# Moving sums, gates, products and evictions by one or two tiles in a kernel with a hand-made order of issue

## The chip, the cores and the metric

One Trainium2 chip, one core of it. The metric is the device time of one execution in microseconds, as the median of several runs. The engines are TensorE (PE, with its weight loads as PEld), VectorE (DVE), ScalarE (ACT), GpSimd (POOL) and SyncE (SP), which issues nearly all DMAs. Each engine works through its own instructions in the order in which the program issued them; between engines there are only semaphores. So the order of issue is a part of the kernel, and it is what changes here.

## What is computed

Four layers follow one another on an image of 4 x 192 x 64 x 64, all in f32. The change touches the first two, which are built around a selective scan (Mamba). Cut to what matters:

```python
# layer 0: tokens of 192 channels, 4096 in each image
xs = layernorm(x.reshape(b, -1, c), ln_g, ln_b)
y1 = mamba(xs, m1...)                  # two mambas over the same tokens,
y2 = mamba(flip(xs, -1), m2...)        # the second with its channels turned round
out = xs + y1 + y2

def mamba(x, ...):                     # 384 inner channels, 16 states
    xc, z = split(x @ in_w.T)
    xc = silu(causal_conv(xc) + conv_b)          # 4 taps (3 in layer 1)
    dt, B, C = split(xc @ x_w.T)
    dt = softplus(dt @ dt_w.T + dt_b)
    h = exp(dt * A) * h + (dt * xc) * B          # over the 4096 tokens
    y = sum(h * C, states) + D * xc
    return (y * silu(z)) @ out_w.T

# layer 1
x1 = x + mamba(layernorm(x))
x2 = x1 + gelu(batchnorm(depthwise3x3(x1)))
out = x2 + mlp(layernorm(x2))                    # 192 -> 768 -> 192, gelu
```

Layers 2 and 3 (a convolution with weights from a squeeze, windows multiplied in sedenions, an MLP) come after and are untouched.

## The kernel before

**Units, halves, tiles.** The tokens are worked in chunks of 512. In the first stage (`two_mambas`, layer 0) a unit is one chunk of one image, 32 units in all, and each has two halves, one for each mamba. In the second stage (`mamba_block`, layer 1) a unit has one mamba. For one mamba and one chunk, 384 channels times 16 states give 48 scans of 128 x 512, and these are the tiles: 12 groups k of 4 tiles j. A tile is one `tensor_tensor_scan` on VectorE (L636), for which ScalarE makes the decay `dA` two tiles ahead (L630, three buffers in PSUM). For each group there is a product dtx * B before the scans (L623: on VectorE, but on GpSimd for groups 3, 7 and 11 of the first stage, the `shared` ones, whose B is a copy in SBUF named Bs), and afterwards a product h * C on GpSimd (L649, in `read`).

**What follows the scans.** `sum` (L653) adds the 16 states up with four products into one PSUM tile `y` (L658); four groups make one `y` of 128 channels, c = k // 4, and there is a single buffer for it (`psum_y`). In the first stage the fourth sum also adds D * xc (L668), and `Mamba.skip` then is the gate: it multiplies `y` with silu(z) on VectorE into `m_y` (L681), and `Mamba.gate` does nothing. In the second stage `skip` adds D * xc (L683) and `gate` multiplies on GpSimd. `Scans.step` enters these for later tiles with `at(...)` (L776 to L783), counted from the last tile of a group. With the third gate of a half `gated` is set, and after the second mamba the output products (`back`, L877) are added.

**Work behind the scans.** All the rest, the norms, the fronts of the next unit, the outputs, the depthwise convolution and the MLP, is issued in small pieces between the tiles by `Behind`. Four lanes hold generators; at each tile `tick` lets the lanes go on as far as the rules allow. A `Piece` says what its step costs TensorE (`pe`, taken from a budget that grows by a fixed price for each tile), how many tiles must pass first (`wait`), which other steps must be done (`after`), whether it takes one of the two PSUM banks (`bank`), and whether it is a `burst`: one long activation with another function table, which is let in only at an edge, a tile whose number is 1 modulo 4 and that is not followed by a shared group's product. What empties a bank is entered with `later` and issued some tiles afterwards:

```python
    def later(self, fn, dve=False, bank=True, more=0, act=0.65):
        done = [False]
        due = self.now + (self.dve if dve else self.act) + more
```

The first stage has `Behind(psum, 1.6, 2, 3, 1.0)`: a TensorE budget of 1.6 us a tile, evictions on ScalarE two tiles later, on VectorE three, and 1.0 us of ScalarE's time a tile. The second has `Behind(psum, 1.8, 1, 2, 1.4)` (L1019). Where something is needed and not yet issued, `force` issues everything at once until it is there: `rows` (dt and dt * xc written to DRAM, from where SyncE loads them spread over the partitions), C and Bs, `silu`, `y_free`.

**A front** (`Mamba.front`, L462) is the chain of one mamba and chunk: products `ps_in`, the convolution, a burst silu(xc) (L488), the products `ps_x` (L489 to L492), `ps_dt`, a burst softplus (L512), dt and dt * xc to DRAM, the products for z and a burst silu(z) (L530). A lane works one front after the other, each during the half before its own.

**The norm of the first stage** (`norm` in `two_mambas`, L834) makes 12 short passes on ScalarE (L845) with a few small steps on GpSimd between, then transposes on TensorE (`ps_t`, L863) into `xT`, which has two buffers. `back` of the unit before still reads the older one. It starts once `last`, the output of the unit before (`added`), is done (L916 to L918).

**Second stage:** `NormT.run` (L302) makes a norm with products for mean and variance and a product that spreads 1/sigma (`rb`), multiplied in on VectorE (L347). `MlpT.run` (L366) makes six hidden products, a burst gelu and two outputs of six products (`ps_o`), which VectorE adds to the image (`last`, L1150). `tail` (L1103) makes the depthwise convolution as 18 products (`ps_dw`, L1115) with an eviction on ScalarE (L1124) for each of two halves of the channels and then a burst gelu (L1134).

Of the kernel before, what the change touches and what calls it, by code (L numbers as in the profile page):

```python
# [285 lines left out]
class NormT:  # L286
# [15 lines left out]
    def run(self, x, g, b, d, which):  # L302
        nc, behind = self.nc, self.behind
        nq = T // 128
        mean = behind.bank([CP, T], "mean")
        for k in range(2):
# [5 lines left out]
            dve=True,  # L312
# [25 lines left out]
        for q in range(nq):  # L338
# [10 lines left out]
            ),  # L349
            dve=True,  # L350
        )
        for k in range(2):
# [6 lines left out]
class MlpT:  # L359
# [6 lines left out]
    def run(self, x, taken, last):  # L366
# [22 lines left out]
        for k in range(2):  # L389
            for m in range(NH):  # L390
                if m % 2 == 0:
                    yield Piece(1.7, bank=m == 0, wait=0 if m or k else 2)
                if m == 0:
                    ps = behind.bank([CP, T], "ps_o")
                nc.tensor.matmul(  # L395
                    ps,
                    self.w2[:, m, bass.ts(k, CP)],
                    h[:, m, :],
                    start=(m == 0),
                    stop=(m == NH - 1),  # L400
                )
            h_last = behind.later(lambda k=k, ps=ps: last(k, ps), dve=True)
        yield Piece(after=[h_last])
# [15 lines left out]
class Mamba:  # L419
# [42 lines left out]
    def front(self, xn, first, u):  # L462
# [25 lines left out]
        nc.scalar.activation(xc, xc, AF.Silu)  # L488
        yield Piece(2.6, bank=True, wait=2)  # L489
        ps = behind.bank([RK + 2 * NS, T], "ps_x")  # L490
# [111 lines left out]
    def spread_C(self, u, o):  # L602

        for n, i in (("C", 2 + o), ("Bs", o)):
            if n == "Bs" and not any(k % 2 == o for k in self.shared):
                return
            if n == "Bs":
                yield Piece(0.85, bank=True)
            v = self.work.tile([128, T], F32, name=f"{n}{o}", bufs=2 if n == "C" else 1)
            ps = self.behind.bank([128, T], f"ps_{n}")  # L610
            self.nc.tensor.matmul(ps, self.ex.spread[:, i, :], u["dbl"], start=True, stop=True)
            done = self.behind.later(lambda v=v, ps=ps: self.nc.scalar.copy(v, ps))  # L612
            yield Piece(after=[done])
            u[n, o] = v
# [79 lines left out]
class Scans:  # L694
# [21 lines left out]
    def run(self):  # L716
# [10 lines left out]
        for i in range(self.AHEAD):  # L727
            m.decay(u, 0, i)
        for i in range(n + 16):
            if i < n:  # L730
                self.step(i, n)
            for fn in self.due.pop(i, []):
                fn()
            self.behind.tick(self.edge(i + self.AHEAD, n))
# [6 lines left out]
    def step(self, i, n):  # L741
# [24 lines left out]
        if j == 3:  # L766
# [5 lines left out]
            if i + 1 < n:  # L772
                m2, u2, k2, _ = self.tile(i + 1)
                if k2 not in m2.shared:
                    m2.product(u2, k2)
            late = 2 if m.shared else 0  # L776
            self.at(i + 4 + late, lambda: self.sum(m, u, k))
            if k % 4 == 3:
                c = k // 4
                self.at(i + 6 + late, lambda: self.skip(m, u, c))  # L780
                self.at(i + 8, lambda: m.gate(u, c))
                if c == ND - 1:
                    self.at(i + 8, lambda: self.gated(u, after))  # L783

# [17 lines left out]
def two_mambas(tc, x, gb_ap, m_ins, ex_aps, out, at_first):  # L802
# [3 lines left out]
    with ExitStack() as ctx:  # L806
# [26 lines left out]

        def norm(u):  # L834
            xt = u["x"]
# [23 lines left out]
            for k in range(2):  # L859
                yield Piece(1.1, bank=True, wait=1)  # L860
                ps = behind.bank([CP, T], "ps_t")
# [49 lines left out]
        for n, u in enumerate(units):  # L911
            following = units[n + 1] if n + 1 < len(units) else None

            def before(i, n=n, u=u, following=following):
                if i == 0 and following:
                    load(following)  # L916
                    last = [units[n - 1]["added"]] if n else []
                    behind.add(3, norm(following), Piece(wait=3, after=last))  # L918
                if following:
# [76 lines left out]
def mamba_block(tc, x, p96, p96_ap, p128, p128_ap, m_in, ex_aps, out, sums, following):  # L996
# [4 lines left out]
    with ExitStack() as ctx:  # L1001
# [16 lines left out]

        behind = Behind(psum, 1.8, 1, 2, 1.4)  # L1019
        ln = NormT(nc, const, work, behind)  # L1020
# [82 lines left out]
        def tail(b, t):  # L1103
# [4 lines left out]
            for k in range(2):  # L1108
                for j in range(9):
                    if j % 3 == 0 and (j or k):  # L1110
                        yield Piece(2.6, bank=j == 0)
                    if j == 0:
# [16 lines left out]
                            bias=bn_t[:, k : k + 1],  # L1129
                        )  # L1130
                    )
# [699 lines left out]
```

## Time and profile before

| | us |
|---|---|
| median of 9 runs | 10762.62 (10743.57 to 10771.31) |
| the profiled execution: its time | 10761.38 |
| its span, first to last instruction | 10759.3 |
| first stage, two mambas on each chunk | about 0 to 5380 |
| second stage, one mamba, convolution, MLP | about 5380 to 8830 |
| layers 2 and 3 | to the end |

Busy times by stage (us in the stretch; clock is the share of TensorE's full clock that was granted):

| stretch | PE | DVE | ACT | POOL | clock |
|---|---|---|---|---|---|
| 200 to 5380 (5180 us) | 4215.7 | 4932.3 | 3489.9 | 4658.2 | 0.80 |
| 5700 to 8600 (2900 us) | 2627.4 | 2571.6 | 1997.5 | 2063.4 | 0.88 |
| 8900 to 10760 (1860 us) | 1565.8 | 945.9 | 738.6 | 197.8 | 0.91 |

The stages are so regular that a gap on an engine comes back in each unit at the same place. A group of instructions is read as: line, engine, operation, what it writes and reads, count, then busy time, mean ns of one, and the engine's idle time just before these instructions with what ended it.

### The profile page before, as it was taken

The page shows a single profiled execution, that of the slowest core. Times are in us where ns is not written, and L with a number is a line of the kernel's source. Part 1 is how long each engine was busy: PE and PEld are TensorE (multiplying, and loading weights), DVE is VectorE, ACT ScalarE, POOL GpSimd, SP SyncE. Part 2 cuts the span into 40 slices and gives each one's busy share as a digit, 9 for nine tenths or more (in the row PEclk, how much of TensorE's full clock was granted, in tenths as well). Part 3 has the DMA queues.
Part 4 walks back from the last instruction along what each step waited for, and adds up shares of the span by engine and source line. Part 5 has one row for each costly group of instructions (what it writes and reads, how often), then busy time and mean ns, then how long its engine had stood idle before and what let it go on. Part 6 is the DMA issues. An engine that isn't in the chain of part 4 may idle for free. (4 is left out here: it accounts for less than half of the span.)

```text
span 10759.3 us, 97520 instructions
## 1 busy us (share of the span) xinstructions
PE 8998.6 (84%) x30776; PEld 3510.5 (33%) x30776; DVE 9037.7 (84%) x7697; ACT 6652.8 (62%) x9626; POOL 7363.4 (68%) x3584
## 2 busy tenths in 40 slices
PE   7888888888888888888668999989999986889898
PEld 2222222222222222222223333333333333455455
DVE  7999999999999999999968888888888875555552
ACT  5666666666666666666546767666666653444433
POOL 6889898988888989889857677767677751111100
PEclk7888787878877878788767888889888887899999
DMA  6666666666666666666545555555555542112110
GB/s 166 173 180 183 173 176 174 184 174 173 180 176 174 176 175 185 172 173 180 156 127 141 142 140 147 141 141 148 135 147 139 145 109 72 43 49 64 43 40 18
DMA packets 969562, 1515.13 MB, mean 141 GB/s; under 512 B 244346, under 2 KB 277150, under 8 KB 968534
## 3 DMA queue, kind: packets, MB, share of 16 engines
q1 hardware_dynamic: 968190, 1505.85, 52.5%
q8 instruction: 245, 4.01, 0.2%
q10 hardware_dynamic: 856, 3.05, 0.1%
q14 instruction: 271, 2.22, 0.1%
HBM read 1295.45 MB, written 213.12 MB: 140 GB/s over the span
## 5 line engine op out<-in xcount | busy, mean ns | idle before, releaser
L636 DVE TENSOR_TENSOR_SCAN h<-dA,m_state,h 128x512 f32<-128x512 f32 x3840 | 4659.6, 1266 | 378.7 <-ACT dA L630 310.0
L649 POOL TENSOR_TENSOR h<-h,C 128x2048 f32<-128x2048 f32 x960 | 4348.6, 4530 | 77.7
L630 ACT ACTIVATE dA<-dtE,m_A 128x512 f32<-128x512 f32 x4608 | 3086.5, 686 | 1300.9 <-DVE h L636 1193.5
L623 DVE TENSOR_TENSOR h<-dtxE,B 128x2048 f32<-128x2048 f32 x960 | 2171.1, 2262 | 69.9 <-DMA dtxE<-r_dtx 69.9
L658 PE MATMUL y<-h,gather 128*32 128x512 f32 x7680 | 1266.7, 739 | 461.4 <-POOL h L649 276.1
L474 PE MATMUL ps_in<-xT,m_in_w 96*128 96x512 f32 x1536 | 1109.7, 866 | 193.7 <-ACT z L481 171.6
L1366 POOL TENSOR_TENSOR d<-d,rs 128x512 f32<-128x512 f32 x64 | 86.4, 1350 | 1600.4 <-DVE rs L1365 1579.9
L648 POOL COPY m_state<-h 128x4 f32<-128x4 f32 x960 | 183.1, 191 | 1161.6 <-DVE h L636 1152.1
L636 DVE TENSOR_TENSOR_SCAN h_apart<-dA,m_state,h_apart 128x512 f32<-128x512 f32 x768 | 924.3, 1260 | 39.8 <-ACT dA L630 39.7
L623 POOL TENSOR_TENSOR h_apart<-dtxE,Bs 128x2048 f32<-128x2048 f32 x192 | 882.4, 4596 | 36.7 <-ACT Bs L612 29.2
L649 POOL TENSOR_TENSOR h_apart<-h_apart,C 128x2048 f32<-128x2048 f32 x192 | 869.7, 4529 | 15.5
L548 PE MATMUL ps_conv<-raw,m_conv 128*128 128x512 f32 x1536 | 720.9, 612 | 0.0
L474 PEld LDWEIGHTS ps_in<-xT,m_in_w 96*128 96x128 f32 x1536 | 375.9, 267 | 942.7 <-issue 407.0
L1115 PE MATMUL ps_dw<-strip,dw 96*96 96x512 f32 x1152 | 590.6, 662 | 3.4 <-ACT x L1124 0.9
L658 PEld LDWEIGHTS y<-h,gather 128*32 128x32 f32 x7680 | 168.0, 117 | 1283.0 <-POOL h L649 568.7
L474 PE MATMUL ps_in<-xn,m_in_w 96*128 96x512 f32 x768 | 441.0, 719 | 164.4 <-ACT z L481 70.5
L492 PE MATMUL ps_x<-xc,m_pack 128*44 128x512 f32 x576 | 340.8, 739 | 230.2 <-ACT xc L488 190.7
L395 PE MATMUL ps_o<-hid,t 128*96 128x512 f32 x768 | 446.4, 729 | 75.3 <-ACT ln_rs L332 66.1
L1531 PE MATMUL sed_ps<-xn,sed 64*128 64x256 f32 (+3 forms) x2944 | 486.3, 403 | 7.0 <-DVE y L1550 7.0
L630 ACT ACT_TABLE_LOAD x345 | 442.6, 1283 | 14.7 <-DMA dtE<-r_dt 8.6
L548 PEld LDWEIGHTS ps_conv<-raw,m_conv 128*128 128x128 f32 x1536 | 286.6, 195 | 439.3 <-issue 356.1
L376 PE MATMUL ps_h<-xn,t 96*128 96x512 f32 x768 | 394.8, 661 | 30.6 <-ACT hid L381 16.8
(202 smaller groups left out, 12210.9 us busy)
## 6 DMA issues: line engine op xcount, KB each, us to landing
dtE<-r_dt SPq DMA_DIRECT2D x2304, 256.0 KB, 5.1
dtxE<-r_dtx SPq DMA_DIRECT2D x2304, 256.0 KB, 4.3
r_dt<-dt SPq DMA_DIRECT2D x96, 768.0 KB, 4.0
r_dtx<-raw SPq DMA_DIRECT2D x96, 768.0 KB, 6.4
x<-x SPq DMA_DIRECT2D x64, 384.0 KB, 3.9
img<-x SPq DMA_DIRECT2D x28, 512.0 KB, 9.1
xt<-in_x SPq DMA_DIRECT2D x32, 384.0 KB, 6.3
x<-o SPq DMA_DIRECT2D x32, 384.0 KB, 2.6
```

What stands on the lines that cost most here:

```text
L376: nc.tensor.matmul(ps, self.w1[:, k, bass.ts(m, 128)], x[:, k, :], start=(k == 0), stop=(k == 1))
L395: nc.tensor.matmul(ps, self.w2[:, m, bass.ts(k, CP)], h[:, m, :], start=(m == 0), stop=(m == NH - 1),)
L474: nc.tensor.matmul(ps, self.in_w[:, k, bass.ts(e, 128)], xn[:, k, :], start=(k == 0), stop=(k == 1))
L492: nc.tensor.matmul(ps, self.x_w[:, d, :], xc[:, d, :], start=(d == 0), stop=(d == ND - 1))
L548: nc.tensor.matmul(ps, self.conv[:, d, j, :], raw[:, d, j : j + T], start=(j == 0), stop=(j == K - 1))
L623: engine.tensor_tensor(h, u["rows", k // 2, 1], u[B, k % 2].unsqueeze(1).broadcast_to([128, 4, T]), ALU.mult)
L630: self.nc.scalar.activation(dA, u["rows", k // 2, 0][:, j, :], AF.Exp, scale=self.A[:, k, j : j + 1])
L636: self.nc.vector.tensor_tensor_scan(h[:, j, :], u.pop(("dA", k, j)), h[:, j, :], self.state[:, k, j : j + 1], ALU.mult, ALU.add,)
L649: nc.gpsimd.tensor_tensor(h, h, u["C", k % 2].unsqueeze(1).broadcast_to([128, 4, T]), ALU.mult)
L658: self.nc.tensor.matmul(u["ys"][32 * j : 32 * j + 32, :], self.ex.gather[:, i // 2, :], h[:, j, :], start=(i == 0), stop=(i == 3 and not s ...
L1115: nc.tensor.matmul(ps, dw[:, k, j, :], s[:, k, dy : dy + rows, dx : dx + HW], start=(j == 0), stop=(j == 8),)
L1531: nc.tensor.matmul(out, sed[p, int(h is not None), i ^ position(k, s), cols], xn[b, g][p, c, :], start=group(t) not in begun, stop=left[gr ...
```

## The change

Nothing that is computed changes, only where it is issued:

- In the first stage the sum of a group is issued 7 tiles after its last scan (it was 6), the gate 10 (it was 8), and `gated`, which lets the output products and z's buffer go, 10 (it was 8). In the second stage these numbers stay as they were. The loop of tiles runs four turns longer for it.
- `ps_x`, which follows the burst silu(xc), waits 4 tiles in the first stage and 3 in the second (it was 2 in both).
- One tile later are issued: the copies of C and Bs (both stages), the multiplication of `rb` (L347), the two MLP outputs (L1150), the two evictions of the depthwise convolution (L1124). The first output products behind the MLP's gelu wait 3 tiles, not 2.
- The next unit's norm in the first stage starts without waiting for `added`; only its transposes wait for it.
- TensorE's budget for a tile in the second stage is 2.0, it was 1.8.

```diff
@@ NormT.run
                 d, d, rb.unsqueeze(1).broadcast_to([CP, 2, T]), ALU.mult
             ),
             dve=True,
+            more=1,
         )
@@ MlpT.run
-                    yield Piece(1.7, bank=m == 0, wait=0 if m or k else 2)
+                    yield Piece(1.7, bank=m == 0, wait=0 if m or k else 3)
...
-            h_last = behind.later(lambda k=k, ps=ps: last(k, ps), dve=True)
+            h_last = behind.later(lambda k=k, ps=ps: last(k, ps), dve=True, more=1)
@@ Mamba.front
         nc.scalar.activation(xc, xc, AF.Silu)
-        yield Piece(2.6, bank=True, wait=2)
+        yield Piece(2.6, bank=True, wait=3 if self.summed else 4)
@@ Mamba.spread_C
-            done = self.behind.later(lambda v=v, ps=ps: self.nc.scalar.copy(v, ps))
+            done = self.behind.later(lambda v=v, ps=ps: self.nc.scalar.copy(v, ps), more=1)
@@ Scans.run
-        for i in range(n + 16):
+        for i in range(n + 20):
@@ Scans.step
-            late = 2 if m.shared else 0
-            self.at(i + 4 + late, lambda: self.sum(m, u, k))
+            added, skipped, gated = (7, 10, 10) if m.shared else (4, 6, 8)
+            self.at(i + added, lambda: self.sum(m, u, k))
             if k % 4 == 3:
                 c = k // 4
-                self.at(i + 6 + late, lambda: self.skip(m, u, c))
-                self.at(i + 8, lambda: m.gate(u, c))
+                self.at(i + skipped, lambda: self.skip(m, u, c))
+                self.at(i + gated, lambda: m.gate(u, c))
                 if c == ND - 1:
-                    self.at(i + 8, lambda: self.gated(u, after))
+                    self.at(i + gated, lambda: self.gated(u, after))
@@ two_mambas
-        def norm(u):
+        def norm(u, last=()):
...
-                yield Piece(1.1, bank=True, wait=1)
+                yield Piece(1.1, bank=True, wait=1, after=last)
...
-                    behind.add(3, norm(following), Piece(wait=3, after=last))
+                    behind.add(3, norm(following, last), Piece(wait=3))
@@ mamba_block
-        behind = Behind(psum, 1.8, 1, 2, 1.4)
+        behind = Behind(psum, 2.0, 1, 2, 1.4)
...
                             AF.Identity,
                             scale=bn_s[:, k : k + 1],
                             bias=bn_t[:, k : k + 1],
-                        )
+                        ),
+                        more=1,
                     )
                 )
```

## The prediction

> **What bounds the kernel now.** I read the page first: span, busy times, then the slices.
>
> ```profile
> span 10759.3 us, 97520 instructions
> PE 8998.6 (84%) x30776; PEld 3510.5 (33%) x30776; DVE 9037.7 (84%) x7697; ACT 6652.8 (62%) x9626; POOL 7363.4 (68%) x3584
> PE   7888888888888888888668999989999986889898
> DVE  7999999999999999999968888888888875555552
> PEclk7888787878877878788767888889888887899999
> ```
>
> There are three stages. In the first (to about 5380 us) VectorE is the bound, in the second (to about 8830 us) VectorE and TensorE nearly share it, the third is TensorE's and the change doesn't touch it. So what the change can win is VectorE's idle time in the first two stages. The groups by line, for 200 to 5400 us and then for 5700 to 8600 us, give it (last columns: idle time and who ended it):
>
> ```profile
> L636 DVE TENSOR_TENSOR_SCAN h<-dA,m_state,h 128x512 f32<-128x512 f32 x2256 | 2715.5, 1264 | 131.2 <-ACT dA L630 96.5 <-DVE h L623 0.9
> L636 DVE TENSOR_TENSOR_SCAN h_apart<-dA,m_state,h_apart 128x512 f32<-128x512 f32 x752 | 904.9, 1260 | 36.3 <-ACT dA L630 36.3
> L681 DVE TENSOR_TENSOR m_y<-y,z 128x512 f32<-128x512 f32 x189 | 129.6, 686 | 78.6 <-PE y L668 78.6
> ...
> L636 DVE TENSOR_TENSOR_SCAN h<-dA,m_state,h 128x512 f32<-128x512 f32 x1322 | 1624.5, 1269 | 200.5 <-ACT dA L630 171.8 <-DVE h L623 0.9
> L347 DVE TENSOR_TENSOR xn<-xn,rb 96x1024 f32<-96x1024 f32 x54 | 65.5, 1213 | 40.4 <-PE rb L339 40.4
> L1150 DVE SCALAR_TENSOR_TENSOR x<-ps_o,t,x 96x512 f32<-96x512 f32 x52 | 38.8, 747 | 77.5 <-PE ps_o L395 77.5
> ```
>
> First stage: 131.2 + 36.3 + 78.6 = 246 us. Where it sits shows in the timeline of VectorE:
>
> ```profile
> 1011.92 0.68 DVE L681 TENSOR_TENSOR m_y<-y,z 128x512 f32<-128x512 f32 x1
> ...
> 1091.06 0.68 DVE L681 TENSOR_TENSOR m_y<-y,z 128x512 f32<-128x512 f32 x1
> ...
> 1105.33 4.81 DVE L636 TENSOR_TENSOR_SCAN h<-dA,m_state,h 128x512 f32<-128x512 f32 x4 [1.34 <-ACT dA L630]
> ...
> 1132.98 4.81 DVE L636 TENSOR_TENSOR_SCAN h<-dA,m_state,h 128x512 f32<-128x512 f32 x4 [1.37 <-ACT dA L630]
> ...
> 1177.34 0.69 DVE L681 TENSOR_TENSOR m_y<-y,z 128x512 f32<-128x512 f32 x1 [3.74 <-PE y L668]
> ```
>
> A unit is two halves (one per mamba) of 48 tiles, a tile being one scan. From 1011.92 to 1091.06 a half takes 79.14 us without a stall; the last half of the stage, with almost nothing behind it, takes the same (5253.07 to 5332.21). The next takes 86.28 us: it holds the next unit's norm and the output products. Three units last 495 us (the 3.74 us wait comes back at 1672.32), 165.1 each, against 2 x 79.14 = 158.3. So 6.8 us a unit, x 31 = **210 us**, is all that order can win here.
>
> **The change, part by part, first stage.**
>
> *Norm without the output (L834, L860, L918).* The 12 passes on ScalarE no longer wait for `added` (tile 17 of the first half by the last copy at 1107.28); counted out by the waits they fall on tiles 4-7, 12-15 and 21-24. Today one stands directly behind the softplus burst at tile 29 and the next scan waits 1.37; without it that goes: -1.4. Before the burst at tile 13 ScalarE waits 1.16 and 1.49 us for output products; these start two tiles later (gate at +10), so that wait goes, but two passes now stand around this burst: of 0.54 + 1.34 I keep 0.5: -1.4. Their input DMA is issued at tile 0, where it was (median landing 6.3 us, four tiles and a product take 7.1): no cost; if it is late, ScalarE and the dA behind it wait 1 or 2 us per unit.
> With the passes gone from tiles 30-43, the three z evictions come before tile 37, an edge for a burst; today the last (1141.41) just misses it and silu(z) waits for tile 45 (1155.58). The next front then starts eight tiles sooner, as it does in the other half (1228.25), which doesn't stall. That empties TensorE's queue at the half's end, where it is busy without a break from 1152 to 1177, at clock 0.50 up to 1176: the cause of the 3.74.
> *Sums +1, gate +2 (L776-L783).* From the sum to the gate there are three tiles in place of two; the gate's wait is 78.6/31 = 2.5 us a unit, and one more scan (1.27) plus the emptier queue take nearly all: -2.2. The scans behind it (0.53 + 0.98 in this unit, 1.0 in the mean of three) follow: -0.8. Each h is held one tile longer; it is written again five tiles after its sum now, six before: nothing.
> *The wait added*: the next group's first sum waits, in TensorE's order, for the gate, as there is one y. It was two tiles behind the gate and is now one. Behind it stand the front's and output products, their evictions on ScalarE, then dA, then the scan. Unseen cost: nothing, if TensorE is less than about four tiles (three dA and the eviction's own delay) behind; else a 5.25 us stall (3.74 + 0.53 + 0.98). I take 0.4 a unit.
> *ps_x two tiles later (L489), C one (L612).* ps_x waits 5.6 to 5.9 us for silu(xc) at the head of TensorE's queue in the second half; sums can now pass. The chain gets two tiles longer, and softplus keeps tile 29 (halves done at 25 to 28 by my count). C and, behind it, Bs come up to two tiles later, with Bs at the last tile before POOL's product at tile 6; POOL waited 23.6 us for it in all. Cost up to 1.5 on POOL, which is 90% busy (4658 of 5180): 0 to 0.3.
>
> Sum: -1.4 - 1.4 - 2.2 - 0.8 + 0.4 + 0.3 = -5.1 a unit, x 31 = **-158**; bounds -210 (all) and -100 (the two burst waits and a part of the gate's).
>
> **Second stage.** A unit takes 105.81 us (L347 at 6511.84 and 6617.65); the tile price allows TensorE 48 x 1.8 = 86.4, now 96. L347's wait of 1.5, L1150's of 2.22 and 0.47 go one tile of 1.27 later: 1.27 + 1.27 + 0.47 = 3.0 x 31 = 93. The dw eviction (L1124) waits 1.99 on ScalarE ahead of scan stalls of 1.24 and 1.54; up to 1.27 more, 39. But TensorE is busy 2627.4 of 2900 us here, each later eviction holds one of two banks a tile longer, and 0.2 more products a tile deepen its queue, whose lateness is what z (2.77 on ScalarE, then 2.54 on VectorE) waits for. Bounds: -120 and +126 (one more 2.54 + 1.54 per unit, x 31). I take **-58**, under half of 132. Four more turns of the loop (L729) and the third stage: nothing.
>
> By the profiled execution (10761.4 us, 1.2 below the median): 10761 - 158 - 58 = **10,545**.
>
> [...]
>
> **Rivals.** (1) The second stage gives back: z's wait repeats, +126 in place of -58: 10761 - 158 + 126 = 10,729. For it: TensorE 91% busy; against: four evictions move the right way. (2) *Slower: the single y.* TensorE already waits 178.5 us in 74 waits for the gate (2.4 each). If each half starts late by it, at half clock, 62 x 5.25 = 326; less today's gate and following waits (78.6 + 31), less the norm's 87 (2.8 x 31): +129, 10,890. It decides once TensorE is over four tiles late. Against: the sums' own POOL waits (209.5) shrink. (3) It doesn't do what it says: `rows`, Bs and y_free are needed at tiles 36, 6 and 25, within one to four tiles of where they now come; where one is late, everything is issued at once and the new places are void. Then about a quarter of the first stage's gain stays, -40, none of the second: 10,721.
>
> **Numbers.** Forecast 0.52 (own range 10,430 to 10,640: -210 - 120, and -100 - 20); rival 1 0.18, 2 0.15, 3 0.15. 0.2% (21.5 us) is about what this measurement can tell from no change. Faster: 0.52 + 0.13 + 0.07 = 0.72; same: 0.03 + 0.06; slower: 0.02 + 0.15 + 0.02. The range runs to 10,790, which takes in rivals 1 and 3 and leaves the second out.
>
> **What would show it.** Right: L681's wait under 15 us; both halves near 79.5 us; silu(z) at tile 37 in both; L347 and L1150 idle halved. Wrong: "y <- m_y" above 350 us with gate waits; scan idle behind dA over 170 in the first stage or over 200 in the second.

## The result, and the profile after

The changed kernel takes **10,852.5 us** in the median of 10 runs (10,823.4 to 10,862.6), the kernel before 10,765.6 in the median of 31: a ratio of 1.0078 [1.007, 1.0086]. It is slower by 0.8%, where 10,545 and a gain of 2% were forecast. The page of its profiled execution:

```profile
span 10842.3 us, 97311 instructions
...
PE 8821.7 (81%) x30776; PEld 3506.0 (32%) x30776; DVE 9052.4 (83%) x7697; ACT 6642.0 (61%) x9624; POOL 7367.6 (68%) x3584
...
PE   6777877878788778778658888888888886889898
...
DVE  7999999999999999999968888888888875555552
...
PEclk8887888888878878888768898998998997899999
```

VectorE's busy time is what it was (9037.7 before), and the slices look alike: the loss is spread over both stages. Measured from the start of the last gate of the first stage and of the last scan of the second, the first stage went from 5377.6 to 5415.4 us (**+37.8**), the second from 3449.1 to 3492.4 (**+43.3**); the rest stayed (1932.6 and 1934.5).

The groups by line of VectorE, 200 to 5400 us (line numbers from L351 on are one higher than before, from L1132 on two, so L637 is the scan, L682 the gate, L1152 the MLP outputs; kernels with L347 at its old tile have the first shift undone again):

```profile
L637 DVE TENSOR_TENSOR_SCAN h<-dA,m_state,h 128x512 f32<-128x512 f32 x2255 | 2736.9, 1266 | 253.6 <-ACT dA L631 200.6 <-ACT xc L554 0.5 <-DVE h L624 0.5
...
L637 DVE TENSOR_TENSOR_SCAN h_apart<-dA,m_state,h_apart 128x512 f32<-128x512 f32 x748 | 894.6, 1259 | 0.0
L682 DVE TENSOR_TENSOR m_y<-y,z 128x512 f32<-128x512 f32 x188 | 125.5, 668 | 8.2 <-PE ps_out L886 8.2
```

The gate's wait is gone as forecast (78.6 to 8.2), and the shared scans no longer wait (36.3 to 0). But the other scans now wait 253.6 in place of 131.2: the idle time moved to "behind dA". The same view of the second stage, 5700 to 8600 us:

```profile
L637 DVE TENSOR_TENSOR_SCAN h<-dA,m_state,h 128x512 f32<-128x512 f32 x1294 | 1585.6, 1268 | 179.8 <-ACT dA L631 155.8 <-DVE h L624 0.9
...
L309 DVE TENSOR_TENSOR xn<-x,mean 96x1024 f32<-96x1024 f32 x54 | 65.7, 1216 | 87.7 <-PE mean L307 87.7
L347 DVE TENSOR_TENSOR xn<-xn,rb 96x1024 f32<-96x1024 f32 x53 | 63.6, 1199 | 0.0
L684 DVE SCALAR_TENSOR_TENSOR m_y<-xc,m_pack,y 128x512 f32<-128x512 f32 x81 | 59.2, 731 | 40.4 <-PE y L659 40.4
L1087 DVE TENSOR_TENSOR strip<-ps_out,x 96x512 f32<-96x512 f32 x54 | 37.1, 688 | 62.6 <-PE ps_out L1078 62.5
L1152 DVE SCALAR_TENSOR_TENSOR x<-ps_o,t,x 96x512 f32<-96x512 f32 x50 | 36.6, 732 | 0.4 <-PE ps_o L396 0.4
```

Both waits that were to go went (L347 40.4 to 0, the MLP outputs 77.5 to 0.4), and VectorE waits elsewhere for TensorE in their place: L309 0.3 to 87.7, L684 7.7 to 40.4, the strip 2.0 to 62.6. These lines before:

```profile
L309 DVE TENSOR_TENSOR xn<-x,mean 96x1024 f32<-96x1024 f32 x55 | 66.2, 1204 | 0.3
...
L683 DVE SCALAR_TENSOR_TENSOR m_y<-xc,m_pack,y 128x512 f32<-128x512 f32 x83 | 60.1, 725 | 7.7 <-PE y L658 7.7
...
L1086 DVE TENSOR_TENSOR strip<-ps_out,x 96x512 f32<-96x512 f32 x55 | 36.7, 666 | 2.0 <-PE ps_out L1077 2.0
```

In the first stage, the timeline of VectorE over a half without the norm (gate to gate 1025.51 to 1105.22) and the half with it:

```profile
1025.51 0.67 DVE L682 TENSOR_TENSOR m_y<-y,z 128x512 f32<-128x512 f32 x1
...
1105.22 0.67 DVE L682 TENSOR_TENSOR m_y<-y,z 128x512 f32<-128x512 f32 x1
...
1153.99 1.28 DVE L637 TENSOR_TENSOR_SCAN h<-dA,m_state,h 128x512 f32<-128x512 f32 x1 [0.98 <-ACT dA L631]
...
1158.79 2.46 DVE L637 TENSOR_TENSOR_SCAN h<-dA,m_state,h 128x512 f32<-128x512 f32 x2 [1.34 <-ACT dA L631]
...
1176.88 3.63 DVE L637 TENSOR_TENSOR_SCAN h<-dA,m_state,h 128x512 f32<-128x512 f32 x3 [4.43 <-ACT dA L631]
```

Two things are new. The undisturbed half takes 79.71, not 79.14. And at 1176.88 a scan waits 4.43 us, at the place in time of the old gate stall. What is late there is seen on TensorE:

```profile
1136.78 1.98 PE L475 MATMUL ps_in<-xT,m_in_w 96*128 96x512 f32 x4 [0.17 <-ACT xT L868]
1145.04 3.78 PE L475 MATMUL ps_in<-xT,m_in_w 96*128 96x512 f32 x4 [6.28 <-ACT xT L868]
...
1168.94 6.61 PE L549 MATMUL ps_conv<-raw,m_conv 128*128 128x512 f32 x8
```

and on ScalarE, in the same stretch:

```profile
1135.96 0.76 ACT L868 ACTIVATE xT<-ps_t,gb 96x512 f32<-96x512 f32 x1
...
1138.61 1.48 ACT L513 ACTIVATE dt<-dt 128x1536 f32<-128x1536 f32 x1
...
1144.23 0.76 ACT L868 ACTIVATE xT<-ps_t,gb 96x512 f32<-96x512 f32 x1
...
1175.58 0.69 ACT L554 ACTIVATE xc<-ps_conv,m_pack 128x512 f32<-128x512 f32 x1 [5.95 <-PE ps_conv L549]
```

The normed tokens come in two copies. The first `xT` stands before the softplus burst (1138.61), the second is issued four tiles behind it, because the burst has used up the ScalarE time that the planner allows, and starts 5.6 us after the burst does. TensorE waits 6.28 us for it and works on at half speed (four products in 3.78 us against 1.98, at a granted clock of 0.50 from 1144 to 1148); the z evictions come late, and the next half's convolution is still slow at 1168.94 (eight products in 6.61 us, against 3.70 at 1084.46). ScalarE has its eviction `xc` at the head of its queue for 5.95 us with dA behind it, and VectorE waits for that dA.

### The profile page after: what moved, and what is told of

Read it like the earlier page. It is cut to its first block, busy times and chain, and to the rows that moved or that the text cites. A ratio compares the mean times of both kernels' runs of the same rounds, so it can differ in the third digit from the quotient of the medians.

```text
span 10842.3 us, 97311 instructions
## 1 busy us (share of the span) xinstructions
PE 8821.7 (81%) x30776; PEld 3506.0 (32%) x30776; DVE 9052.4 (83%) x7697; ACT 6642.0 (61%) x9624; POOL 7367.6 (68%) x3584
## 3 DMA queue, kind: packets, MB, share of 16 engines
q14 instruction: 271, 2.22, 0.1%
## 5 line engine op out<-in xcount | busy, mean ns | idle before, releaser
L637 DVE TENSOR_TENSOR_SCAN h<-dA,m_state,h 128x512 f32<-128x512 f32 x3840 | 4677.5, 1267 | 476.6 <-ACT dA L631 393.3
L659 PE MATMUL y<-h,gather 128*32 128x512 f32 x7680 | 1195.0, 704 | 498.2 <-DVE m_y L682 370.0
L475 PE MATMUL ps_in<-xT,m_in_w 96*128 96x512 f32 x1536 | 1012.3, 806 | 452.7 <-ACT xT L868 196.0
L637 DVE TENSOR_TENSOR_SCAN h_apart<-dA,m_state,h_apart 128x512 f32<-128x512 f32 x768 | 918.7, 1259 | 3.5 <-ACT dA L631 3.4
L549 PE MATMUL ps_conv<-raw,m_conv 128*128 128x512 f32 x1536 | 796.5, 659 | 0.0
L493 PE MATMUL ps_x<-xc,m_pack 128*44 128x512 f32 x576 | 372.7, 799 | 267.8 <-ACT xc L489 144.1
L1116 PE MATMUL ps_dw<-strip,dw 96*96 96x512 f32 x1152 | 549.1, 627 | 0.0
L475 PE MATMUL ps_in<-xn,m_in_w 96*128 96x512 f32 x768 | 411.4, 677 | 163.3 <-ACT z L482 75.7
L377 PE MATMUL ps_h<-xn,t 96*128 96x512 f32 x768 | 425.8, 698 | 30.6 <-ACT xn L355 15.4
L554 ACT ACTIVATE xc<-ps_conv,m_pack 128x512 f32<-128x512 f32 x192 | 132.2, 688 | 504.6 <-PE ps_conv L549 504.6
```

The lines of the kernel that those rows point to most:

```text
L377: nc.tensor.matmul(ps, self.w1[:, k, bass.ts(m, 128)], x[:, k, :], start=(k == 0), stop=(k == 1))
L475: nc.tensor.matmul(ps, self.in_w[:, k, bass.ts(e, 128)], xn[:, k, :], start=(k == 0), stop=(k == 1))
L493: nc.tensor.matmul(ps, self.x_w[:, d, :], xc[:, d, :], start=(d == 0), stop=(d == ND - 1))
L549: nc.tensor.matmul(ps, self.conv[:, d, j, :], raw[:, d, j : j + T], start=(j == 0), stop=(j == K - 1))
L637: self.nc.vector.tensor_tensor_scan(h[:, j, :], u.pop(("dA", k, j)), h[:, j, :], self.state[:, k, j : j + 1], ALU.mult, ALU.add,)
L659: self.nc.tensor.matmul(u["ys"][32 * j : 32 * j + 32, :], self.ex.gather[:, i // 2, :], h[:, j, :], start=(i == 0), stop=(i == 3 and not s ...
```

## The experiments

Each run was set against these theories. **N**: the early norm itself brings the new stall. **P**: the place of the gate costs time. **X**: the later output products hold `xT` over the softplus burst. **Single y**: the rival of the prediction, the next sum close behind the gate. **A**: in the second stage ScalarE's pass over `xn` (L355) stands behind the later L347.

Since the change has parts for each stage, most kernels try one thing in each. Lengths are from one profile per kernel. A first stage with the same order of issue came out at 5287.4, 5303.1 and 5290.6 (f3, g2, h2), so 15 us is not a finding there; the same second stage came out between 3406 and 3414 six times (f2, g2, h1, h3, h4, i1). "Stalls" are all idle times of VectorE above 0.25 us in its timeline from 200 to 5250 us, added up, each counted once.

| kernel | first stage | stalls in it | second stage | time |
|---|---|---|---|---|
| before | 5377.6 | 203.4 | 3449.1 | 10,765.6 |
| changed | 5415.4 | 206.2 | 3492.4 | 10,852.5 |
| e1 | 5289.0 | 118.6 | 3584.1 | 10,811 |
| e2 | 5399.7 | 170.9 | 3504.6 | 10,884 |
| e3 | 5355.5 | 138.2 | 3807.5 | 11,105 |
| e4 | 5422.0 | 234.3 | 3476.3 | 10,825 |
| f1 | 5408.0 | 203.3 | 3628.8 | 10,973 |
| f2 | 5354.0 | 146.1 | 3413.2 | 10,697 |
| f3 | 5287.4 | 115.1 | 3542.1 | 10,758 |
| f4 | 5419.5 | 212.7 | 3527.7 | 10,881 |
| g1 | 5383.3 | 208.3 | 3449.2 | 10,773 |
| g2 | 5303.1 | 130.8 | 3407.1 | **10,633** |
| g3 | 5301.8 | 101.9 | 3535.9 | 10,762 |
| g4 | 5428.8 | 245.4 | 3420.2 | 10,769 |
| h1 | 5418.3 | 209.3 | 3407.4 | 10,769 |
| h2 | 5290.6 | 121.4 | 3498.5 | 10,726 |
| h3 | 5312.4 | 112.5 | 3407.6 | 10,649 |
| h4 | 5289.0 | 86.1 | 3406.3 | **10,638** |
| i1 | 5497.5 | 284.5 | 3413.0 | 10,839 |

Times of the e and f kernels, g1, g3 and g4 are single runs, and single runs are uncertain: of the kernel before, those beside e and f took 10,808 and 10,810, while the median beside g, on the chip of e, was 10,763. On i1's chip the median of the kernel before was 10,802. So a few tens of us in the e and f kernels show little by themselves; what the argument rests on was repeated in rounds (g2, h1 to h4, i1).

**e1, early norm alone; in the second stage the budget alone.**

```diff
@@ against before
-                    behind.add(3, norm(following), Piece(wait=3, after=last))
+                    behind.add(3, norm(following, last), Piece(wait=3))
...
-        behind = Behind(psum, 1.8, 1, 2, 1.4)
+        behind = Behind(psum, 2.0, 1, 2, 1.4)
```

> The kernel before, with only the early norm of the first stage and only the budget of 2.0 in the second. First stage (to the last gate, 5377.6 us before, 5415.4 after). Theory N, that the early norm brings the new stall (the second transposed tile keeps a bank until the softplus burst is paid off, TensorE then idles about 6 us and falls to half clock): the stall stays here, length 5360 to 5400. Rival G, that the later sums and gates bring it: it is gone, every half runs near 79.5 us, length 5210 to 5290. Second stage (last gate to last scan, 3449 before, 3492 after). Theory B, that the deeper budget slows it: 3490 or more. Rival E, that the later evictions and waits do: 3449 or less.

First stage 5289.0, 89 us under before: the early norm alone wins, and N falls. The budget alone costs 135 in the second stage.

**e2, the changed kernel without the early norm and with the budget of 1.8.**

```diff
@@ against the changed kernel
-                    behind.add(3, norm(following, last), Piece(wait=3))
+                    behind.add(3, norm(following), Piece(wait=3, after=last))
...
-        behind = Behind(psum, 2.0, 1, 2, 1.4)
+        behind = Behind(psum, 1.8, 1, 2, 1.4)
```

> The changed kernel, with the norm of the first stage put back (it waits for the output again) and the budget of the second back at 1.8. First stage: under N the 6 us idle of TensorE before z and the 4.4 us stall go; what is left is the waits of before less that for the gate, plus 0.19 us for each gate that now stands between scans (26.57 in place of 26.38 from gate to gate): 5300 to 5380. Under G it stays at 5410 or more. Second stage: under B it falls to 3380 to 3440; under E it stays near 3490.

5399.7 and 3504.6. It is confounded: counted in the order of issue, this kernel forces Bs and `rows` in every unit of the first stage and `rows` in 24 units of the second, which neither before nor the changed kernel does.

**e3, only the sums and gates (7, 10, 10); in the second stage only L347 and the MLP outputs.**

```diff
@@ against before
-            late = 2 if m.shared else 0
+            added, skipped, gated = (7, 10, 10) if m.shared else (4, 6, 8)
...
+            more=1,
...
+            h_last = behind.later(lambda k=k, ps=ps: last(k, ps), dve=True, more=1)
```

> The kernel before, with only the sums, gates and output products of the first stage later (7, 10, 10), and in the second only the two evictions on VectorE (L347, L1150) one tile later. First stage: theory P, that a gate between two scans costs 0.19 us more than one behind a product: a half without a stall takes 79.71 us, 36 us in all; with the gate's wait of 78.6 us gone but the norm's waits kept, 5330 to 5390. Rival: the half stays at 79.14. Second stage: if these two are what VectorE gains by, 3350 to 3400; if a wait takes their place, 3440 or more.

5355.5: the gates alone win 22, little more than what doesn't repeat. But this is not their price by itself: in the first stage too, counted in the order of issue, `rows` is forced in 30 units, since the softplus burst has slipped from tile 77 of a unit to tile 81, and `rows` is needed at 84. Firmer is the pair in which neither kernel forces more than a unit or two: the early norm alone wins 89, with the later gates added (f1) it loses 30. So the two collide. In the second stage 3807.5: without the larger budget `rows` is forced in 25 units, and in 21 of them VectorE stalls 9.3 to 10.5 us two tiles later. The third rival's mechanism exists, in this part of the change taken alone, not in the whole.

**e4, the changed first stage with the gate back at 8; the second with only bn, C and `ps_x` later.**

```diff
@@ against the changed kernel
-            added, skipped, gated = (7, 10, 10) if m.shared else (4, 6, 8)
+            added, skipped, gated = (7, 8, 10) if m.shared else (4, 6, 8)
```

> First stage of the changed kernel, with the gate alone back at 8 tiles, behind a product again (sums at 7, output products at 10). Theory P: the half without a norm takes 79.14 us again, and the first stage is some 36 us shorter, 5370 to 5390, unless the gate waits again (one tile from its sum): then waits on y of over 80 us show. Rival: it stays at 79.71. Second stage: the kernel before, with the later evictions and waits on ScalarE's side alone (depthwise convolution, C, ps_x): under E slower, 3470 or more; else 3400 to 3450.

Gate to gate without a stall takes 26.38 us again, as before, against 26.57 where the gate is at 9 or 10 (the changed kernel, h1, h3, h4, i1): P's price is there. But one tile behind its sum the gate waits 81.3 us, and Bs is forced in every unit: 5422.0. The second stage forces `rows` in 25 units here too, so its 3476.3 does not tell what the later steps on ScalarE cost.

**f1, early norm and gates without C and `ps_x`; f3, the changed kernel with 6, 8, 8; f4, the changed kernel without the later C.** In the second stage f1 takes `ps_x` back, f3 the wait for `ps_o`, f4 the MLP outputs (L1152).

```diff
@@ f1, against the changed kernel
-        yield Piece(2.6, bank=True, wait=3 if self.summed else 4)
+        yield Piece(2.6, bank=True, wait=2)
...
@@ f3
-            added, skipped, gated = (7, 10, 10) if m.shared else (4, 6, 8)
+            added, skipped, gated = (6, 8, 8) if m.shared else (4, 6, 8)
-                    yield Piece(1.7, bank=m == 0, wait=0 if m or k else 3)
+                    yield Piece(1.7, bank=m == 0, wait=0 if m or k else 2)
@@ f4
-            h_last = behind.later(lambda k=k, ps=ps: last(k, ps), dve=True, more=1)
+            h_last = behind.later(lambda k=k, ps=ps: last(k, ps), dve=True)
...
```

> First stage: the kernel before with the early norm and the later sums, gates and output products (7, 10, 10), but ps_x and C where they were. The early norm alone took 5289 us, the whole change 5415. Theory X: the output products, two tiles later, push the norm's transposes so late that the second transposed tile keeps a PSUM bank through the softplus burst (TensorE then idles some 6 us before the products for z, falls to half clock, and the 4.4 us stall follows). Under X the idle and the stall are here too: 5370 or more. Rival Y: ps_x and C, moved, bring it: 5289 + 36 for the gates' place, less the gate's waits, so 5300 to 5340. Second stage: the changed kernel with ps_x two tiles behind its burst, as before: 3480 to 3500 if it plays no part.

> First stage: the early norm, ps_x two tiles later and C one, with sums, gates and output products where they were before (6, 8, 8). Under X near 5289 (5270 to 5310); under Y 5370 or more. Second stage: the changed kernel, the first products behind the MLP's gelu two tiles later as before: 3480 to 3500 if it plays no part.

> First stage: the changed kernel with C and Bs where they were. Under X 5400 to 5420; if C has a part in the stall, under 5380. Second stage: the changed kernel with the MLP's outputs (L1150) where they were: their waits of 2.69 us a unit return, so 3500 to 3560 if nothing else depends on it; under 3480 if the bank held a tile longer costs more than the wait it removes.

First stage: f1 and f4 are as slow as the changed kernel, f3 as fast as e1. C and `ps_x` play no part; early norm with gates at 10 is the loss. Second stage: each part taken back makes it slower, `ps_x` by 136, the wait by 50, L1152 by 35. None of them is the culprit.

**f2, the copy of `xT` freed of ScalarE's allowance; L347 at its old tile.**

```diff
@@ against the changed kernel
-            more=1,
...
                         xT[:, k, :], ps, AF.Identity, scale=gb[:, k, 0:1], bias=gb[:, k, 1:2]
-                    )
+                    ),
+                    act=0,
```

> First stage: the changed kernel, only that the copy of the transposed tile (xT, L868) no longer waits for ScalarE's allowance after a burst. Under X the idle of 6 us before z goes and the first stage falls to 5240 to 5340; under Y it stays at 5390 or more. Second stage: the changed kernel with the multiplication of rb (L347) back where it was. Theory A: moved one tile later without the affine pass behind it (L355, still three tiles after the product), it leaves ScalarE waiting for VectorE in the same tile (194.6 us of waits, 65.7 before), and dA stands behind. Under A these waits fall below 90 and the stage to 3430 to 3460; rival: the waits go elsewhere, 3480 or more.

First stage 5354.0: 61 less than the changed kernel, above the band that X gave, so the copy's hold is a part and not all (the table by place below shows which). Second stage 3413.2, better than A's band: undoing this one move wins 79 and leaves it 36 under before.

**g1, before once more; g2, the changed kernel with two steps undone.** g2 has 6, 8, 8 (as f3) and L347 at its old tile (as f2), all else as changed.

> The kernel before once more, on the chip of these experiments, so that the lengths of its stages there are known: this chip's total is 0.4% above the first one's, so by both theories 5377 to 5410 for the first stage (last gate), 3449 to 3475 for the second (last gate to last scan).

> The changed kernel with two parts undone: sums, gates and output products of the first stage back at 6, 8, 8, and L347 back where it was. Under theory X (late output products) and theory A (L347 without its affine pass): first stage 5287, second 3413, as these were in two other kernels, so some 10,630 in all, 1.6% below the kernel before on the same chip. If the parts of the two stages don't add up: above 10,700.

g1 shows how far one profile repeats (5383.3 and 3449.2). g2 takes 10,633, a ratio to before of 0.9876 [0.986, 0.9893].

**g3, sums at 8, so that two tiles lie between gate and next sum, and `xT` free; in the second stage L347 and L1152 back.**

```diff
@@ against the changed kernel, with the edit of f2 for xT
-            added, skipped, gated = (7, 10, 10) if m.shared else (4, 6, 8)
+            added, skipped, gated = (8, 10, 10) if m.shared else (4, 6, 8)
```

> First stage: the changed kernel, xT free of ScalarE's allowance, and the sums at 8, so that the next group's first sum stands two tiles behind the gate again, not one. With xT free alone it took 5354. If the single y held TensorE up (rival 2 of the prediction): the 2.84 us stall at the start of the second half goes and the waits on y for the gate fall below 200 us, 5270 to 5310. If not: 5345 to 5365. Second stage: the changed kernel with L347 and L1150 both where they were: L1150's waits return, 3440 to 3500 (3413 with L347 alone put back).

5301.8, 52 under f2, as the single y would have it; but TensorE still waits 344 us for the gate, where under 200 was expected. So the sum's tile matters. The total hides a shift: at the first gate of the second half TensorE's wait falls from 131.3 us (f2) to 27.3, at the third gates of the two halves it rises from 87.6 and 89.8 to 150.2 and 143.1. Which of this spares VectorE its stalls isn't shown. With L347 back, the later L1152 is worth some 125 (3535.9 against 3406 to 3414).

**g4, early norm alone with its transposes held two tiles; L347 and the two evictions of the convolution back.**

```diff
@@ against e1
-                yield Piece(1.1, bank=True, wait=1, after=last)
+                yield Piece(1.1, bank=True, wait=1 if k else 3, after=last)
```

> First stage: the kernel before with the early norm alone (5289), and its transposes held back by two tiles, as late output products do. Under X TensorE idles again before the products for z (PE ps_in waiting for xT over 100 us in all) and the stage takes 5340 to 5420; if something else of the gates' move was the cause, 5285 to 5300. Second stage: the changed kernel with L347 and the depthwise evictions (L1124) where they were: 3413 if the latter play no part, above 3440 if they help.

5428.8, 140 over e1, with gates at 8: late transposes alone undo the early norm. They do it by another door, since here silu(z) slips to tile 45 and the gate waits 87.1. The evictions of the convolution play little part (3420.2 against 3406 to 3414).

**h1 to h4, in rounds.** h1 undoes only L347's move, h2 only the sums and gates (6, 8, 8). h3 is g3's first stage with f2's second. h4 has everything one tile later than before (7, 9, 9), and L347 back.

```diff
@@ h4, against the changed kernel
-            more=1,
...
-            added, skipped, gated = (7, 10, 10) if m.shared else (4, 6, 8)
+            added, skipped, gated = (7, 9, 9) if m.shared else (4, 6, 8)
```

> The changed kernel with one step undone: L347 goes at its old tile again. First stage untouched. Theory (ScalarE's affine pass stands behind L347 in the same tile): only the second stage gets shorter, 3492 to about 3410, so about 10,770 in rounds (10,755 to 10,785), level with the kernel before. Rival (the loss of the second stage came from the deeper TensorE queue, and L347's part depended on what else was undone with it): 10,820 or more.

> The changed kernel with the sums and gates of the first stage at 6, 8, 8 again, all else as changed. Theory: the first stage falls from 5415 to 5287 to 5303 (no price of the place, no xT held over the burst, the two-tile gap between gate and next sum), the second stays at about 3492: 10,730 (10,715 to 10,750). If the two steps undone act on one another, it is 20 or more away from that, and with the run that undoes only L347's move the savings do not add up to the 219 us that the version with both undone saves.

> Gates at 10 as changed, but with the sum at 8 (two tiles between the gate and the next sum), the copy of xT let out without counting against ScalarE's allowance, and L347 at its old tile. Theory: with its two late waits mended, the later gate costs only its place: first stage about 5302, total 10,640 (10,625 to 10,660). Rival (late gates cost more than these two waits): 10,680 or more.

> Sums at 7, gates and what they let go at 9 (one tile later than before, all gaps between sum, gate and next sum as before), early norm, L347 at its old tile. Theory: the gate stands between two scans and costs its place, 0.19 us each, 36 in all: 10,633 + 36 = 10,669 (10,655 to 10,690), gate to gate 26.57 us without a stall. Rival 1 (place costs nothing in the end, other idle time takes it): 10,635. Rival 2 (output products one tile later already hold xT over the softplus burst): stalls behind dA of over 3 us in the first stage again, 10,700 or more.

h1: 1.0011 [1.0001, 1.002], h2: 0.9971 [0.9959, 0.9982], h3: 0.9897 [0.9883, 0.9912], h4: 0.9888 [0.9873, 0.9903]. Undoing the two steps one by one wins 84 and 126, 210 in sum, and both together (g2) 219: they add up, as nearly as chips agree. h4 is not the 10,669 expected. Its gates do cost 26.57 apiece, but its stalls are 86.1 where g2 has 130.8, and that pays for the place. Against h1 it differs by one tile of the gate and of what it lets go: **129 us** of first stage.

**i1, as h4, but the output products at 10.**

```diff
@@ against h4
-            added, skipped, gated = (7, 9, 9) if m.shared else (4, 6, 8)
+            added, skipped, gated = (7, 9, 10) if m.shared else (4, 6, 8)
```

> As h4 (sum at 7, gate at 9, early norm, L347 at its old tile), but what the third gate lets go, the output products and z's buffer, one tile later, at 10 as in the changed kernel. It parts the two waits of the tenth tile. Theory: the gap between gate and next sum stays two tiles, so the starts of the halves stay as in h4, but the output products and behind them xT come late again: about 60 us over h4, first stage about 5350, total 10,700 (10,680 to 10,720), TensorE waiting over 100 us for xT. Rival 1 (the gap alone did it): 10,638, as h4. Rival 2 (the late output products alone did it): all 129 us back, 10,767.

1.0034 [1.0021, 1.0046], first stage 5497.5: by the ratios 1.46% or 157 us over h4, with two tiles between gate and next sum in both. So the price of the tenth tile lies in the output products, more than twice the 60 us that X had given it, and the narrow gap is not needed for the stall. (z's buffer is let go at the same tile, but in the program only the products behind the softplus burst, some 20 tiles later, ask for it.) ScalarE in h4, and then in i1, at the same point of a unit:

```profile
1127.96 0.76 ACT L867 ACTIVATE xT<-ps_t,gb 96x512 f32<-96x512 f32 x1
...
1129.23 0.77 ACT L867 ACTIVATE xT<-ps_t,gb 96x512 f32<-96x512 f32 x1
...
1131.89 1.48 ACT L512 ACTIVATE dt<-dt 128x1536 f32<-128x1536 f32 x1
```

```profile
1131.85 0.76 ACT L867 ACTIVATE xT<-ps_t,gb 96x512 f32<-96x512 f32 x1
...
1134.50 1.48 ACT L512 ACTIVATE dt<-dt 128x1536 f32<-128x1536 f32 x1
...
1140.12 0.76 ACT L867 ACTIVATE xT<-ps_t,gb 96x512 f32<-96x512 f32 x1
```

With the products at 9 both copies come before the burst, at 10 the second falls behind it, as in the changed kernel. The waits of TensorE in i1, 200 to 5400 us (total, times, longest), name it; in h4 the second of them is 0.5 us in all:

```profile
PE y L658 <- DVE m_y L681: 226.6, 92, 4.1
PE ps_in L474 <- ACT xT L867: 223.2, 60, 6.3
```

## Why the prediction was wrong, point by point

**First stage, the sum.** Length and stalls close: 5377.6, plus the difference in stalls to before, plus 36 us where the gate stands between two scans, gives the measured first stage within 8 us for all kernels but five (9 to 19 off for e2, e4, g3, g4 and h3). For the changed kernel: 206.2 - 203.4 + 36 = +38.8, measured +37.8. The forecast of -158 needed the stalls to fall to about 45. Where they sit, by VectorE's timelines (us in total, 30 or 31 units; tiles are counted through a unit, 0 to 95):

| stalls | before | e1 | changed | f2 | h4 |
|---|---|---|---|---|---|
| behind the burst silu(xc) at tile 13 | 44.7 | 64.8 | 9.0 | 9.0 | 11.7 |
| behind the softplus burst at tile 29 | 41.5 | 0 | 0 | 18.7 | 0 |
| first half's last gate and behind it | 96.9 | 0.9 | 0 | 0 | 0 |
| behind the burst silu(z) at tile 37 | 0 | 0 | 63.6 | 0 | 0 |
| start of the second half | 0.5 | 6.5 | 80.8 | 21.0 | 38.8 |
| start of the first half | 11.2 | 29.2 | 43.8 | 76.8 | 33.1 |
| elsewhere | 8.6 | 17.2 | 9.0 | 20.6 | 2.5 |

In the changed kernel the first three rows fall by 174 us, and -1.4 - 1.4 - 2.2 - 0.8 over 31 units are 180: what the sum booked as gains came. The next three rows grow by 176, and 36 for the gate's place come on top; for these the sum had 0.7 a unit. So most of the signs of being right came (the gate's wait under 15 us, silu(z) at tile 37 in both halves, L347 and the MLP outputs with less than half their idle time): they watched the gains. Of the signs of being wrong, the scans' wait for dA in the first stage came, 200.6 where over 170 was named.

- *"these start two tiles later (gate at +10), so that wait goes"*: **the step that failed.** That wait did go (first row), but the later output products were booked as a gain only. The new norm's transposes wait for that very output, so its second copy slid over the softplus burst, where ScalarE's allowance held it, and TensorE waits 196.0 us for it. f2, which frees the copy alone, has no stall behind silu(z) at tile 37 and a quarter of the one at the second half's start. That silu(z) stands at tile 37 costs nothing by itself: in e1, f2 and h4 it is there too. But f2 has more stalls at the first half's start, and the sum of all this, the price of one tile, is what h4 against h1 (129) and i1 (157) measure.
- *Norm without the output, -1.4 and -1.4 a unit*: alone it wins 87 to 90 (e1, f3, h2; 75 in g2), and 2.8 x 31 is 87, but that they agree is luck. Alone it takes away the stalls at tile 29 as forecast, makes those at tile 13 longer, and removes the gate's wait nearly whole, which the forecast had given mostly to the gate's own tile.
- *Gate's wait, -2.2*: it goes, 78.6 to 8.2 is 2.3 a unit, though by e1 the early norm is enough for it. silu(z) does come at tile 37 in both halves, as forecast (here at 1155.27). It did not empty TensorE's queue at the half's end in the changed kernel.
- *The gate's place at nothing*: mis-sized. Behind a product it adds 0.42 us to the chain (1009.75 to 1012.53 before, 2.78, against 2.36 from product to scan), between two scans 0.19 more (26.57 against 26.38 from gate to gate): x 192 gates = 36. h4 shows that it need not decide.
- *The single y, 0.4*: one sign that I had named came (TensorE's waits for the gate 178.5 to 368.3), the gate waits that go with it did not. It is not the cause of the loss: e1 waits 306.6 and is faster than before, i1 waits 226.6 and is slower than the changed kernel. What the sum's eighth tile does in g3 and h3 stays open.
- A small slip: three units in 495 us are 165.0 each, so order could win 208 and not 210; nothing rests on it.

**Second stage, -58.** "L347's wait of 1.5, L1150's of 2.22 and 0.47 go one tile later" came true on VectorE: 117.5 of idle time left these two lines. Missing was what stands behind L347: ScalarE's pass over `xn` (L355) follows in the tile to which L347 has now moved, and dA stands behind that pass. The timeline of the changed kernel, VectorE and ScalarE:

```profile
6578.02 0.75 DVE L684 SCALAR_TENSOR_TENSOR m_y<-xc,m_pack,y 128x512 f32<-128x512 f32 x1 [2.20 <-PE y L659]
...
6578.69 1.21 DVE L347 TENSOR_TENSOR xn<-xn,rb 96x1024 f32<-96x1024 f32 x1
...
6579.93 1.52 ACT L355 ACTIVATE xn<-xn,t 96x512 f32<-96x512 f32 x2 [4.56 <-DVE xn L347]
```

L347 stands behind scans and a wait for `y`, and ScalarE waits 4.56 us for it, with evictions and dA queued. Over the stretch from 5700 to 8600 (waits of ScalarE):

```profile
ACT xn L355 <- DVE xn L347: 194.6, 52, 5.0
```

Before:

```profile
ACT xn L354 <- DVE xn L347: 65.7, 26, 2.6
```

In h1 it is 93.8. With only that move undone the second stage takes 3407.4, 42 under before, and the waits of VectorE that had grown shrink again (L309 to 13.2, L683 to 4.7, the strip to 31.9): the rest of the sum had the right sign, and the gain is seven tenths of the 58. The larger budget is needed for it: without it the later evictions force `rows` (e3), and without them it costs 135 (e1).

**The rivals.** The first (second stage gives back) was right about the place and not the cause, which wasn't z but `xn`; it had the first stage's gain standing. The slower one, the single y, had the end right and the mechanism wrong. The third holds in e2 to e4 only. The range's top, 10,790, left the second out, and the time was beyond it.

**What it would have been.** With both steps mended, h4 and g2 take 10,638 and 10,633. What h4 lacks to the forecast lies mostly in the first stage (-89 in place of -158), less in the second (-43 in place of -58).

## What to carry to other kernels

When a step is moved later, follow what waits for it through the planner's rules to the next fixed point (here a burst), and not only through the engine's queue: one tile too many cost 129 us here. When a producer moves by a tile, move its consumer on the other engine too, or that engine's whole queue waits: ScalarE's waits for L347 went from 65.7 to 194.6 us here. And try the parts of such a change by themselves and in pairs: the early norm won 89 by itself and lost 30 with the later gates, which by themselves (with `rows` forced) had won 22.

## What the runs showed of the hardware

The place of a VectorE instruction of 0.67 us among scans has a price: 26.38 us from gate to gate where it stands behind a 128x2048 product, 26.57 where it stands between two scans, in the undisturbed stretches (the first in before, g2, g4 and h2, the second in the changed kernel, h1, h3, h4 and i1).

After 6.28 us without a product TensorE's next four took 3.78 us in place of 1.98; the clock granted went from 1.00 to 0.59 and 0.50 (the column behind the busy times of PE, PEld, DVE, ACT and POOL):

```profile
1136.00:1140.00 4.00, 2.59 (x12) 0.68 (x4) 4.00 (x5) 3.97 (x5) 4.00 (x1) 1.00 1.06 266
1140.00:1144.00 4.00, 0.00 (x0) 0.00 (x0) 3.90 (x3) 3.69 (x6) 3.92 (x4) 0.59 0.80 261
1144.00:1148.00 4.00, 2.96 (x4) 1.18 (x4) 4.00 (x4) 2.66 (x5) 4.00 (x1) 0.50 0.99 265
```

In the kernel before, TensorE's clock was 1.00 in the microsecond from 1135, and after 2.47 us without a product it was 0.50 in the one from 1137:

```profile
1136.73 3.78 PE L474 MATMUL ps_in<-xT,m_in_w 96*128 96x512 f32 x4 [2.47 <-ACT z L481]
```

Over the first stage no loss of clock shows: from 200 to 5380 us TensorE's idle times of 2.47 us and more went from 154 to 220, while its busy time fell, from 4215.7 to 4069.9, and its granted clock was 0.80 before and 0.81 after.
